# Attention's second product in a cross-attention kernel: matmuls of 256 columns in place of 512

## The chip, the cores and the metric

The kernel runs on one core of a Trainium2 chip. A core has a matrix engine (PE, with its weight loads PEld shown apart), a vector engine (DVE), an activation engine (ACT), a general engine (POOL) and a queue for transfers (SP). Matrix products are written to eight accumulator banks of 128 rows by 512 fp32 columns; ACT and DVE read them from there. The metric is the time of one execution on the device in microseconds (us), the median over runs. Lower is better.

## What is computed

Two batches of 2048 tokens with 640 channels attend to 154 context tokens (77 of text, 77 of an image prompt), with 20 heads of 32 channels. Text and image each have their own keys, values and softmax, and the two outputs are added.

```
q = split_heads(x @ Wq.T)
k, v       = split_heads(text @ Wk.T), split_heads(text @ Wv.T)
k_ip, v_ip = split_heads(ip @ Wk_ip.T), split_heads(ip @ Wv_ip.T)
out = softmax(q k.T / sqrt(32)) v + softmax(q k_ip.T / sqrt(32)) v_ip
return merge_heads(out) @ Wo.T + bo + x
```

All of it is in fp32.

## The kernel before, in words

Four heads of 32 channels fill the 128 rows of a tile, so 20 heads make five groups; with two batches there are ten pairs of batch and group, numbered q = 0 to 9. A pair's 2048 tokens fall into two halves (`sub` 0 and 1) of 1024.

For each half the kernel projects queries (line 194), multiplies them with the keys (line 226), copies the scores from the banks into a large buffer `pb` (ACT, line 238), and does the softmax there: maxima (DVE, line 251), subtraction (line 265), exponential (ACT, line 272), sums (DVE, line 297), division (line 309). Then DVE transposes `pb` in blocks of 32 by 32 (line 316). `pb` has three zones of 1024 tokens: an even q has its halves in zones 0 and 1, an odd q in zones 2 and 1.

When both halves of a pair are transposed, `attend` (line 318) multiplies the probabilities with the values. Text and image tokens stand behind each other, 154 rounded up to 160, that is five blocks of 32 (`NK` = 5). The matmuls use 32 by 32 pieces of PE's array, called squares here: a square is one (r, g) with r the row group of the array that it reads from (which also names the bank) and g the head, which names the 32 output rows. For each block k, all 16 squares (r, g) are issued, each with its own 32 by 32 weights from `v4` and 512 columns of `pb`, 256 of them from each of the pair's two zones. A result adds up over the five k in its bank. That is 80 matmuls an attend, and ten attends. ACT then copies the four banks to `aT` (lines 348 and 352), and PE multiplies with the output weights: for the first batch by a scheme with seven products (lines 464 to 493), for the second by one with products on sums of blocks (line 854, after the last attend).

The order of all work on all engines is written out by hand: a long list of words, one for each step, and each engine takes its instructions in the order of that list. `A.8@1360` is the attend of pair 8 on banks 1, 3, 6 and 0. The list is not touched by the change. Waits between engines are placed by the framework from what each instruction reads and writes.

In the trace every fp32 matmul of the program stands as two weight loads (LDWEIGHTS on PEld) and two matmul records on PE: an attend's 80 matmuls are 160 records, the ten attends 1600. The two are called a square's first and second pass here; both use the same 32 by 32 piece of the array, and both read the same columns.

Of the kernel before, what the change touches and what calls it, by code (L numbers as in the profile page):

```python
# [15 lines left out]
H, D, TEXT = 20, 32, 77  # L16
# [4 lines left out]
def kernel(  # L21
# [25 lines left out]
    nc = tc.nc  # L47
# [3 lines left out]
    G = P // D  # L51
    TB = 512
    NH = 2
    BLK = NH * TB
    NT = BLK // P
    SUB = S // BLK
    NHB = SUB * NH
# [3 lines left out]
    NK = (2 * L + D - 1) // D  # L61
    LP = NK * D
    SCALE = 1.0 / float(D) ** 0.5
    NP = B * NC
# [17 lines left out]
    v4s = [const.tile([P, G, NK, D], F32, name=f"v4_{n}") for n in range(2)]  # L82
# [235 lines left out]
    def attend(q, pa):  # L318

        zones = pb[:, ds(q % 2, SUB)].rearrange("p z n g (k s) -> p (z n) g k s", k=NK)  # L320
        for k in range(NK):
            for r in range(G):
                rows = slice(r * D, (r + 1) * D)
                for g in range(G):
                    nc.tensor.matmul(  # L325
                        pa[r][g * D : (g + 1) * D, :],
                        v4s[q % 2][rows, g, k, :],
                        zones[rows, :, g, k, :],
                        start=(k == 0),
                        stop=(k == NK - 1),  # L330
                    )

    def rows_of_attention(b, c):

# [304 lines left out]
    def emit(word):  # L639
# [8 lines left out]
        elif k == "A":  # L648
            at[name] = banks_at(where)
            attend(x, at[name])  # L650
        elif k == "CA":
            take_attention(x, at[f"A.{x}"])
# [244 lines left out]
```

## Time and profile before

| | |
|---|---|
| time, median of 3 runs | 498.39 us (498.36 to 498.49) |
| span of the profiled execution, first to last instruction | 496.5 us |
| PE busy | 489.3 us (99%) |
| DVE busy | 441.2 us (89%) |
| POOL busy | 403.7 us (81%) |
| ACT busy | 241.9 us (49%) |
| line 325, the attends on PE | 55.2 us busy, 1600 records |
| chain that ended last, PE's share | 91% |

The page gives no other time of the profiled execution than its span; it lies 1.9 us under the median of the timed runs, and what is outside the first and last instruction is taken as unchanged. PE's records have real starts, while their ends are modelled, so the starts are what to read. A row of a table of stretches gives, for each engine, the busy time within the stretch and in brackets how many instructions overlap it; where all stretches begin just before an attend, the number in brackets counts what has started by the stretch's end.

### The profile page before, as it was taken

How to read it: one execution, taken by the hardware profiler on the slowest of the kernel's cores; microseconds unless marked ns; L12 is line 12 of the kernel's file. 1: busy time of each engine (PE TensorE's matmuls, PEld its weight loads, DVE VectorE, ACT ScalarE, POOL GpSimd, SP SyncE). 2: the span in 40 equal slices, each digit the busy share in tenths (PEclk: the TensorE clock that was granted, in tenths of full speed). 3: DMA queues.
4: the chain of work that ended last, by engine and by line, in shares of the span. 5: the costliest groups of instructions: out<-in, count | busy, mean ns of one | idle time of the engine just before them, and what ended most of it. 6: DMA issues, size and time to landing. Idle time of an engine off the chain costs nothing.

```text
span 496.5 us, 9743 instructions
## 1 busy us (share of the span) xinstructions
PE 489.3 (99%) x4114; PEld 288.0 (58%) x4114; DVE 441.2 (89%) x404; ACT 241.9 (49%) x423; POOL 403.7 (81%) x173
## 2 busy tenths in 40 slices
PE   8999999999999999999999999999999999999996
PEld 4658548648647556456655655744766575444442
DVE  0078999999989989998999998899899999999886
ACT  1277557757747567567506635545764443100000
POOL 0079959999989999997995899799599999378770
PEclk9999999999999999999999999999999999999999
DMA  8980542511843735715577078345515012510026
GB/s 291 354 213 20 153 107 71 176 51 36 209 133 89 244 108 172 219 16 164 222 243 237 22 241 309 97 150 185 189 65 160 3 45 64 170 62 24 0 106 232
DMA packets 66956, 70.15 MB, mean 141 GB/s; under 512 B 3680, under 2 KB 46688, under 8 KB 66912
## 3 DMA queue, kind: packets, MB, share of 16 engines
q1 hardware_dynamic: 65648, 67.96, 44.0%
q10 hardware_dynamic: 1264, 1.57, 0.9%
q8 instruction: 32, 0.52, 0.4%
q14 instruction: 12, 0.10, 0.1%
HBM read 58.21 MB, written 11.30 MB: 140 GB/s over the span
## 4 chain that ended last, share of the span: by engine, by line
PE 91%; DVE 6%; DMA 1%; ACT 1%; ACTq 0%; issue 0%; DVEq 0%
PE bank L194 35%; PE bank L854 11%; PE bank L325 11%; PE bank L226 10%; PE bank L133 9%; PE bank L483 9%; PE bank L464 4%; PE bank L493 2%; DVE pb L316 2%; DMA x<-in_x_dram 1%; DVE den L297 1%; DVE mx L251 1%; DVE acc L508 0%; DVE acc L512 0%; ACT pb L238 0%
## 5 line engine op out<-in xcount | busy, mean ns | idle before, releaser
L309 POOL TENSOR_TENSOR pb<-pb,rden 128x1848 f32<-128x1848 f32 (+1 forms) x59 | 172.1, 2938 | 24.0 <-DVE rden L304 21.2
L265 POOL TENSOR_TENSOR pb<-pb,mx 128x1848 f32<-128x1848 f32 (+1 forms) x55 | 162.8, 2977 | 35.4 <-DVE mx L251 35.2
L194 PE MATMUL bank<-x,wq 128*128 128x512 f32 x400 | 178.6, 598 | 0.9 <-DMA wq<-in_L_xattn_Wq_dram 0.6
L251 DVE TENSOR_REDUCE mx<-pb 128x24 f32<-128x1848 f32 (+1 forms) x60 | 109.3, 1841 | 31.5 <-ACT pb L238 31.3
L194 PEld LDWEIGHTS bank<-x,wq 128*128 128x128 f32 x400 | 74.0, 190 | 89.3 <-issue 82.0
L238 ACT COPY pb<-bank 128x462 f32<-128x462 f32 (+1 forms) x240 | 102.0, 537 | 44.5 <-PE bank L226 43.9
L272 ACT ACTIVATE pb<-pb 128x1848 f32<-128x1848 f32 (+1 forms) x60 | 94.3, 1584 | 55.0 <-POOL pb L265 54.2
L297 DVE TENSOR_REDUCE den<-pb 128x24 f32<-128x1848 f32 (+1 forms) x60 | 110.0, 1840 | 5.9 <-ACT pb L272 5.7
L316 DVE STREAM_TRANSPOSE pb<-pb 128x1920 f32<-128x1920 f32 (+1 forms) x60 | 113.9, 1923 | 0.9 <-POOL pb L309 0.9
L226 PEld LDWEIGHTS bank<-kT,qT 32*128 32x128 f32 x1280 | 45.9, 184 | 23.6 <-issue 14.2
L226 PE MATMUL bank<-kT,qT 32*128 32x154 f32 x1280 | 56.5, 305 | 1.0 <-ACT pb L238 0.7
L325 PE MATMUL bank<-pb,v 32*32 32x512 f32 x1600 | 55.2, 597 | 0.1
L204 ACT ACTIVATE qT<-bank 128x512 f32<-128x512 f32 x40 | 23.6, 597 | 50.3 <-PE bank L194 50.3
L133 PE MATMUL bank<-wo_ct,aT 128*128 128x154 f32 x320 | 45.5, 296 | 0.0
L133 PEld LDWEIGHTS bank<-wo_ct,aT 128*128 128x128 f32 x320 | 43.0, 188 | 3.6 <-issue 2.7
L325 PEld LDWEIGHTS bank<-pb,v 32*32 32x32 f32 x1600 | 29.5, 103 | 22.9 <-issue 11.7
L464 PE MATMUL bank<-aT,wo_ct 128*128 128x512 f32 x80 | 36.3, 596 | 0.0
L483 PE MATMUL bank<-aT,wo_ct 128*128 128x256 f32 x128 | 32.8, 389 | 0.0
L802 DVE TENSOR_TENSOR x<-x,bank 128x512 f32<-128x512 f32 x36 | 23.6, 684 | 5.2 <-PE bank L854 4.6
L483 PEld LDWEIGHTS bank<-aT,wo_ct 128*128 128x128 f32 x128 | 23.3, 190 | 6.4 <-issue 3.7
L464 PEld LDWEIGHTS bank<-aT,wo_ct 128*128 128x128 f32 x80 | 15.0, 190 | 17.3 <-issue 17.1
L854 PE MATMUL bank<-pb 128*128 128x512 f32 x48 | 22.1, 593 | 0.0
(74 smaller groups left out, 347.6 us busy)
## 6 DMA issues: line engine op xcount, KB each, us to landing
x<-in_x_dram SPq DMA_DIRECT2D x20, 1280.0 KB, 7.7
out_dram<-acc SPq DMA_DIRECT2D x20, 256.0 KB, 2.6
acc<-in_x_dram SPq DMA_DIRECT2D x16, 256.0 KB, 4.0
x<-in_x_dram SPq DMA_DIRECT2D x15, 256.0 KB, 5.7
out_dram<-x SPq DMA_DIRECT2D x15, 256.0 KB, 2.0
v<-scr SPq DMA_DIRECT2D x40, 80.0 KB, 4.1
wq<-in_L_xattn_Wq_dram SPq DMA_DIRECT2D x9, 320.0 KB, 5.3
aT<-in_L_xattn_Wk_dram SPq DMA_DIRECT2D x5, 512.0 KB, 6.9
```

Of the source, the lines that this page charges most:

```text
L133: nc.tensor.matmul(keys_in(out), loaded[n][:, k, :], cT[:, k, :, t, :], start=(k == 0), stop=(k == NCC - 1))
L194: nc.tensor.matmul(pq, wqs[q % 3][:, k, :], xs[place_of(u, h)][:, k, :], start=(k == 0), stop=(k == NC - 1),)
L226: nc.tensor.matmul(ps[g][:, ts(t, 2 * L)], qTs[(u, h)][g * D : (g + 1) * D, ts(st, P)], kT[g * D : (g + 1) * D, c, b].rearrange("p t l -> ...
L238: nc.scalar.copy(keys_of(u, s)[:, :, g], ps[g][:, : n * 2 * L].rearrange("p (n l) -> p n l", n=n))
L251: nc.vector.tensor_reduce(mx, rows_of(u, s), AX.X, ALU.max, negate=by_rows(u, s))
L265: eng.tensor_tensor(rows_of(u, s), rows_of(u, s), maxs[(u, s)].unsqueeze(3).to_broadcast([P, n, 2, L]), ALU.subtract)
L272: nc.scalar.activation(e, e, AF.Exp)
L297: nc.vector.tensor_reduce(dens[(u, s)], rows_of(u, s), AX.X, ALU.add)
L309: eng.tensor_tensor(rows_of(u, s), rows_of(u, s), rdens[(u, s)].unsqueeze(3).to_broadcast([P, n, 2, L]), ALU.mult)
L316: nc.vector.transpose(p, p)
L325: nc.tensor.matmul(pa[r][g * D : (g + 1) * D, :], v4s[q % 2][rows, g, k, :], zones[rows, :, g, k, :], start=(k == 0), stop=(k == NK - 1),)
L483: nc.tensor.matmul(part, w_of[m][:, kp, op], t_of(m, b, i)[:, kp], start=(op == kp == 0 and m in (1, 2, 5)), stop=(op == 1 and kp == 1 and ...
```

## The change

Only `attend` is changed. A matmul now covers 256 columns in place of 512: one half h of the bank, which is one zone of `pb`. An attend has 160 matmuls in place of 80, over the same columns in all, with the weights of a square given again for the second half. There are three orders. For even q except 8, all 16 squares (r outside, g inside) go on half 0 and then all 16 on half 1, for each k. For odd q it is the same, with r inside and g outside. For q = 8 (`NP - 2`) both halves of one square follow each other before the next square. Only the first matmul of a square in an attend (k = 0, h = 0) starts a new sum in the bank; the second half is opened by it as well.

```
     def attend(q, pa):
         zones = pb[:, ds(q % 2, SUB)].rearrange("p z n g (k s) -> p (z n) g k s", k=NK)
+        span = NHB * TB // G // NH
+        part = SUB * NT // NH
+
+        def square(k, h, r, g):
+            rows = slice(r * D, (r + 1) * D)
+            nc.tensor.matmul(
+                pa[r][g * D : (g + 1) * D, ds(h * span, span)],
+                v4s[q % 2][rows, g, k, :],
+                zones[rows, ds(h * part, part), g, k, :],
+                start=(k == h == 0),
+                stop=(h == NH - 1 and k == NK - 1),
+                skip_group_check=True,
+            )
+
         for k in range(NK):
-            for r in range(G):
-                rows = slice(r * D, (r + 1) * D)
-                for g in range(G):
-                    nc.tensor.matmul(
-                        pa[r][g * D : (g + 1) * D, :],
-                        v4s[q % 2][rows, g, k, :],
-                        zones[rows, :, g, k, :],
-                        start=(k == 0),
-                        stop=(k == NK - 1),
-                    )
+            if q == NP - 2:
+                for r in range(G):
+                    for g in range(G):
+                        for h in range(NH):
+                            square(k, h, r, g)
+                continue
+            for h in range(NH):
+                for r in range(G):
+                    for g in range(G):
+                        square(k, h, *((g, r) if q % 2 else (r, g)))
```

On PE, at the first attend (q = 0, `v_0` holds its values, the banks are named by number), the start of the block k = 0 read before, behind the query projection of line 194:

```order
L194 MATMUL bank_80<-x_97,wq_88 128x512 x5
L325 MATMUL bank_86<-pb,v_0_92 32x512 x4
L325 MATMUL bank_83<-pb,v_0_92 32x512 x4
L325 MATMUL bank_84<-pb,v_0_92 32x512 x4
L325 MATMUL bank_85<-pb,v_0_92 32x512 x4
```

and now, where the matmul is on line 326:

```order
L194 MATMUL bank_80<-x_97,wq_88 128x512 x5
L326 MATMUL bank_86<-pb,v_0_92 32x256 x4
L326 MATMUL bank_83<-pb,v_0_92 32x256 x4
L326 MATMUL bank_84<-pb,v_0_92 32x256 x4
L326 MATMUL bank_85<-pb,v_0_92 32x256 x4
L326 MATMUL bank_86<-pb,v_0_92 32x256 x4
L326 MATMUL bank_83<-pb,v_0_92 32x256 x4
L326 MATMUL bank_84<-pb,v_0_92 32x256 x4
L326 MATMUL bank_85<-pb,v_0_92 32x256 x4
```

Four squares (the four g) on each bank came once for a block k; now the round over the four banks comes twice, once for each half. What stands before the attend and behind it is the same.

At the attend of q = 8, behind an output product (line 464 before, 479 now), the block k = 0 read before:

```order
L464 MATMUL bank_86<-aT,wo_ct 128x512 x5
L325 MATMUL bank_80<-pb,v_0_92 32x512 x4
L325 MATMUL bank_82<-pb,v_0_92 32x512 x4
L325 MATMUL bank_85<-pb,v_0_92 32x512 x4
L325 MATMUL bank_79<-pb,v_0_92 32x512 x4
```

and now:

```order
L479 MATMUL bank_86<-aT,wo_ct 128x512 x5
L326 MATMUL bank_80<-pb,v_0_92 32x256 x8
L326 MATMUL bank_82<-pb,v_0_92 32x256 x8
L326 MATMUL bank_85<-pb,v_0_92 32x256 x8
L326 MATMUL bank_79<-pb,v_0_92 32x256 x8
```

Each bank is visited once for a block k as before, with eight matmuls in place of four: two in a row on each of its four squares.

## Prediction

> **What bounds the kernel now.** I read the page first, then the waits of PE, then stretches.
>
> ```profile
> span 496.5 us, 9743 instructions
> PE 489.3 (99%) x4114; PEld 288.0 (58%) x4114; DVE 441.2 (89%) x404; ACT 241.9 (49%) x423; POOL 403.7 (81%) x173
> PE 91%; DVE 6%; DMA 1%; ACT 1%; ACTq 0%; issue 0%; DVEq 0%
> L325 PE MATMUL bank<-pb,v 32*32 32x512 f32 x1600 | 55.2, 597 | 0.1
> ```
>
> PE is busy 99% of the span and holds 91% of the chain that ended last. Its modelled ends can hide waits, so I ask what ended its idle times; the first row of PE's waits is the longest, and of the attends' weight loads only three waited for a transpose:
>
> ```profile
> PE bank L546 <- DVE pb L544: 1.1, 1, 1.1
> PEld bank L325 <- DVE pb L316: 2.0, 3, 1.0
> ```
>
> By stretches, from the first attend to the last one, and within it the two behind the attend of q = 8 (columns: PE, PEld, DVE, ACT, POOL busy; clock; transfers):
>
> ```profile
> 69.00:426.40 357.40, 357.23 (x3407) 217.84 (x3406) 340.31 (x282) 208.07 (x356) 323.37 (x126) 1.00 0.46 141
> 391.00:399.00 8.00, 8.00 (x192) 5.47 (x169) 7.90 (x11) 5.29 (x9) 7.77 (x5) 1.00 0.02 5
> 399.00:426.40 27.40, 27.34 (x126) 17.08 (x124) 27.23 (x27) 8.79 (x13) 26.20 (x15) 1.00 0.24 78
> ```
>
> PE idles 0.17 us of 357.40, at full clock. So whatever an attend gains or loses on PE moves everything behind it one for one. From 399.00 DVE is full too (27.23 of 27.40), and the chain of waits goes over to it there; but PE is as full, so a later PE has nothing to be absorbed in.
>
> **What sets the time of an attend.** First the price of one pass. In the chain of waits, 20 records of 512 columns take 8.58 us and 8 of 256 columns 1.73 us, that is 0.429 and 0.216 each: a pass costs its columns, with nothing fixed.
>
> ```profile
> 46.82 8.58 PE bank L194 x20
> 365.89 1.73 PE bank L483 x8
> ```
>
> An attend has 160 passes on 16 squares, so 10 sets of 16; at 0.429 these are 4.29 us. Measured is more, from PE's timeline:
>
> ```profile
> 69.03 5.52 PE L325 MATMUL bank<-pb,v 32*32 32x512 f32 x160
> 74.48 1.07 PE L226 MATMUL bank<-kT,qT 32*128 32x154 f32 x24
> ```
>
> From its first start to the next line's are 5.45 us, 1.16 over the ten sets. The stretches of line 325 show where that goes (PE, then PEld; in brackets the starts so far; all counted from 69.02):
>
> ```profile
> 69.02:69.47 0.45, 0.43 (x16) 0.31 (x32) 1.00 0.00 0
> 69.02:69.60 0.58, 0.56 (x25) 0.42 (x33) 1.00 0.00 0
> 69.02:69.90 0.88, 0.86 (x32) 0.42 (x33) 1.00 0.00 0
> 69.02:70.10 1.08, 1.06 (x33) 0.52 (x34) 1.00 0.00 0
> 69.02:70.12 1.10, 1.08 (x34) 0.54 (x35) 1.00 0.00 0
> 69.02:70.33 1.31, 1.29 (x47) 0.74 (x60) 1.00 0.05 14
> 69.02:71.17 2.15, 2.13 (x66) 1.12 (x68) 1.00 0.24 66
> 69.02:71.19 2.17, 2.15 (x67) 1.14 (x69) 1.00 0.25 69
> 69.02:72.26 3.24, 3.23 (x101) 1.85 (x103) 1.00 0.54 158
> 69.02:73.34 4.32, 4.30 (x135) 2.61 (x137) 1.00 0.71 198
> 69.02:73.95 4.93, 4.92 (x159) 2.91 (x160) 1.00 0.74 200
> 69.02:73.97 4.95, 4.93 (x160) 2.91 (x160) 1.00 0.73 200
> ```
>
> By 69.47 sixteen passes and 32 weight loads have started: I read the first pass of all 16 squares, with the weights of the second passes loaded behind. By 69.90 the 16 second passes have started too. Then nothing, though 15 squares have room for their next weights: 33 loads and 32 matmuls are in, and only when the first square has ended both passes (2 x 0.429, at 69.92) does one more matmul start, and the 34th start comes at 70.11. So PE looks ahead over 16 squares and no further. From then the starts come in steps: 34, 67, 101 and 135 by 70.12, 71.19, 72.26 and 73.34, that is 34 starts, or **17 squares, every 1.073 us**. One step is a square's two passes, 0.858, plus a **pause of 0.215** until the square 17 places behind it has got in. Within a step squares follow each other closely (13 starts from 70.12 to 70.33, 0.0165 each). Check: first late start 1.075 after the first; three more steps, 4.295 (square 68 of 0 to 79); eleven squares at 0.0165, 4.48; the last square's second pass 0.429 and 0.022 later, 4.93. The table has the last start between 73.95 and 73.97, 4.93 after 69.03. Behind the last start the pass (0.429) and 0.088 go by until line 226.
>
> **The change part by part.** Columns stay the same: twice as many passes of half the length. What doubles is the number of squares that pass through a lookahead that counts instructions. The weights of all added squares are loaded again; the loads hide, as before, behind the passes (33 were in while 32 passes ran).
>
> *Nine attends (all but q = 8).* A step of 17 squares is now 2 x 0.216 + 0.215 = 0.647, and there are 160 squares. First late start: 1.075 less 2 x 0.213 = 0.649. Eight more steps reach square 153 at 5.825; six squares at 0.0165, 5.92; the last one's second pass 0.216 + 0.022 later, **6.16** against 4.93, so +1.23. Behind it the shorter last pass gives back 0.429 - 0.216 = 0.213. Net **+1.02 each, +9.17 in all**. Steps of issue do not bind: 17 squares at 0.0165 are 0.28 of 0.647. The swapped order for odd q changes which square is 17 places behind, not that it is a different one, so I price it at nothing.
>
> *The attend of q = 8.* Two squares in a row use the same piece, so four passes queue on it, 4 x 0.216 = 0.864, and 16 squares of lookahead fill only 8 pieces. A step is 0.864 + 0.215 = 1.079 and moves 18 squares. First late start at about 1.08; seven more steps reach square 144 at 8.63; 14 squares, 8.86; the last piece's fourth pass starts 3 x 0.216 + 0.022 later, 9.53. Against 4.93 that is +4.60, less 0.213: **+4.39**.
>
> *Waits.* An even q's half 0 needs only one zone, so 16 squares can start before the other half's transpose. Three waits of 2.0 us together, which include 0.5 that PE needs to empty before any attend, leave some 0.5 us that this could save at most; I take 0. The transfers of `v4` are waited for by the first squares as before. What is late next: the copies out of the banks and line 226, each by what the attend adds.
>
> *Sum.* 9.17 + 4.39 = 13.56. On the span 496.5 it gives 510.1; with the 1.9 us outside it, 498.39 + 13.56 = **512.0**.
>
> *Bounds.* The unknown is the pause at 256 columns. Its lower bound is nothing: then 0.649 + 8 x 0.647 loses 9 x 0.215, and an attend is 0.92 faster than before (break-even of a normal attend at 0.102). Its upper bound is the full 0.215, seen in all steps at both places where it can be read (the end of the first square and three steps later). I take 0.215, since it begins when a pass has ended and holds no column time.
>
> [...]
>
> **Rivals.**
>
> *A fixed price for each set of 16 passes.* The 1.16 us over ten sets may be 0.116 a set, whatever its order. Twenty sets of 0.332 are 6.64, +1.19 an attend, all ten alike: +11.9, **510.3**. For it: it needs no lookahead. Against: the steps of 34 starts, not 32. Chance 0.15, with all cases in which q = 8 costs about as much as the others.
>
> *The lookahead holds columns, not instructions (faster).* Place: the stop at 69.60 to 69.92. If what is full there is a store of pending columns, 32 squares of 256 fit, and a step of 34 squares costs 4 x 0.216 + 0.215 = 1.079, as 17 do now. Then only the last pass is shorter: 10 x -0.213 = -2.1, **496.3**. It decides as soon as the pause per 17 squares falls under 0.102; with none at all it would be 9 us. Against: 33 loads, 64 instructions and one, is a count of instructions. Chance 0.11.
>
> *The pair of q = 8 blocks what stands behind it.* If a second square on a busy piece stops all issue until the first has ended, each of the 80 pairs costs 2 x 0.216 or more: 34.6 us in place of 5.45, +29, **537**. For it: the trace never has two matmuls in a row on one piece. Against: second passes did wait 0.429 while squares behind them started. Chance 0.10.
>
> *One start every 0.0165 is all that binds.* 320 starts take 5.3: +0.37 - 0.213, +0.16 an attend, **500**. Against: by 69.47 and 69.60 starts come closer (9 in 0.13). Chance 0.08. That the change does nothing measurable: 0.05.
>
> **How the numbers follow.** The forecast has 0.51, with a range of its own from 509 to 515. Within about 0.2% (1 us) this kernel cannot be told from unchanged; that is the 0.05. Faster is the 0.11; slower the rest, 0.84. The range leaves out the blocked pair and the faster case: from the rival of starts, 500, to where the pair of q = 8 costs some 12 us in place of 4.4, **500 to 520**.
>
> **What would show it.** Right: nine attends of 6.5 us from first start to the next line's; in them 34 starts every 0.65 us; q = 8 at about 9.8; PE still idle under 1 us from the first attend to the last. Wrong: attends under 5.45 (lookahead in columns); all ten at 6.6 (a price a set); q = 8 above 20 (blocked); odd q apart from even q (the swapped order costs something that I have at nothing); or PE waiting for DVE between attends, by which part of the loss would be absorbed.

## The result and the profile after

The changed kernel takes **538.16 us** (median of six runs), the kernel before 498.38 on the same chip: a ratio of 1.0795, with a 95% interval of 1.0775 to 1.0814. The ratio leaves out one run of 545.83 us, in which the granted clock was lower (0.981, against 0.989 to 0.994 in the others). The changed kernel is slower by some 40 us. The forecast was 512.0, with a range of 500 to 520: the direction was right, the size missed by more than the range.

The page of the changed kernel, in the profiled execution (536.72 us, with the span below):

```profile
span 534.8 us, 12947 instructions
PE 509.8 (95%) x5714; PEld 311.1 (58%) x5714; DVE 439.6 (82%) x404; ACT 242.5 (45%) x423; POOL 403.8 (76%) x173
q8 instruction: 45, 0.74, 0.6%
PE 94%; issue 3%; DMA 1%; ACT 0%; ACTq 0%; DVE 0%
L326 PE MATMUL bank<-pb,v 32*32 32x256 f32 x3200 | 73.6, 390 | 16.5 <-issue 16.4
```

PE still sets the end, but it is no longer busy all the time, and the attends' row now has idle time, 16.4 us of it with the releaser "issue": PE stood still and waited for nothing that the profile names. Before, that row had 0.1. The first rows of PE's waits say the same with counts (us in total, times, longest):

```profile
PE bank L326 <- issue: 16.4, 11, 3.2
PE bank L226 <- issue: 1.4, 2, 0.7
```

PE's timeline shows where they lie. In such a row the x counts the starts up to the next stop, and the idle time in brackets stands ahead of the row. It runs from the modelled end of the last pass; from start to start a stop is up to 0.4 us longer. The attends of q = 3, 5, 6, 7, 8 and 9:

```profile
188.67 4.02 PE L326 MATMUL bank<-pb,v 32*32 32x256 f32 x192
192.93 2.75 PE L326 MATMUL bank<-pb,v 32*32 32x256 f32 x128 [0.24 <-issue]
...
272.41 2.81 PE L326 MATMUL bank<-pb,v 32*32 32x256 f32 x135
277.05 2.74 PE L326 MATMUL bank<-pb,v 32*32 32x256 f32 x128 [1.83 <-issue]
281.33 1.43 PE L326 MATMUL bank<-pb,v 32*32 32x256 f32 x57 [1.53 <-issue]
...
320.33 4.68 PE L326 MATMUL bank<-pb,v 32*32 32x256 f32 x229
328.18 2.08 PE L326 MATMUL bank<-pb,v 32*32 32x256 f32 x91 [3.18 <-issue]
...
366.92 4.08 PE L326 MATMUL bank<-pb,v 32*32 32x256 f32 x201
373.55 4.01 PE L326 MATMUL bank<-pb,v 32*32 32x256 f32 x119 [2.55 <-issue]
...
417.25 9.99 PE L326 MATMUL bank<-pb,v 32*32 32x256 f32 x320
...
457.18 3.95 PE L326 MATMUL bank<-pb,v 32*32 32x256 f32 x184
463.95 2.75 PE L326 MATMUL bank<-pb,v 32*32 32x256 f32 x128 [2.82 <-issue]
467.68 0.63 PE L326 MATMUL bank<-pb,v 32*32 32x256 f32 x8 [0.98 <-issue]
```

Every normal attend has one or two such stops; q = 8 has none. Where two follow within an attend, they are 128 starts apart (q = 5: after 135 and 263), and a start on PE goes with a weight load (5714 of each on the page), so they are 256 instructions apart. Counted in the order of PE's instructions through the whole program (loads, matmuls, and the waits that stand as instructions of their own), the stops of all attends lie on one lattice of 256: each lies 193 or 194 instructions past a multiple of 256. The page's queue q8, of the kind "instruction", has packets of 16 KB (0.74 MB in 45). Before, the row was

```profile
q8 instruction: 32, 0.52, 0.4%
```

The change adds 3200 instructions (1600 matmuls and 1600 loads) and 13 packets. If a packet holds 256, these are 3328; run 5 below, with 6400 instructions and 25 packets more, gives just 256. The trace also has the time of every packet. Before each of the 13 stops of the two rows of waits one packet starts, and PE goes on 2.31 to 2.64 us after that start: at q = 6 the packet starts at 325.70 and PE goes on at 328.18. So the reading is: **PE runs out of instructions at the end of a block of 256 and waits until the next one has come.**

Between the stops the kernel does what the forecast said. Stretches of line 326 from the start of q = 3 (PE, with the starts so far in brackets):

```profile
188.66:189.33 0.67, 0.66 (x34) 1.00 0.00 0
188.66:189.96 1.30, 1.29 (x67) 1.00 0.00 0
188.66:191.91 3.25, 3.24 (x170) 1.00 0.02 5
188.66:192.90 4.24, 4.02 (x192) 1.00 0.01 4
```

34 starts come every 0.65, as forecast (0.647), up to 170; then the count stays at 192 until 192.93.

Where the 38.3 us between the two spans (534.8 and 496.5) are: the ten attends, each from its first start to the next line's, are longer by 36.0 together (7.2 to 8.1 us for q = 0 to 4 and 9.9 to 11.8 for q = 5 to 9, against 5.5). Of that 13.6 is the forecast's sum, and **22.4 are stops and what they bring**. The other 2.3 lie between the attends: a stop just behind q = 0 (1.05) and a low clock behind q = 9 (1.7), less 0.4 by which two other stretches are shorter.

### The profile page after: what moved, and what is told of

Same layout as the page of the kernel before. It is cut to its first block, busy times and chain, and to the rows that moved or that the text cites. A ratio compares the mean times of both kernels' runs of the same rounds, so it can differ in the third digit from the quotient of the medians.

```text
span 534.8 us, 12947 instructions
## 1 busy us (share of the span) xinstructions
PE 509.8 (95%) x5714; PEld 311.1 (58%) x5714; DVE 439.6 (82%) x404; ACT 242.5 (45%) x423; POOL 403.8 (76%) x173
## 4 chain that ended last, share of the span: by engine, by line
PE 94%; issue 3%; DMA 1%; ACT 0%; ACTq 0%; DVE 0%
PE bank L194 32%; PE bank L326 14%; PE bank L869 11%; PE bank L226 10%; PE bank L498 10%; PE bank L133 8%; PE bank L479 7%; PE bank L508 3%; DMA wq<-in_L_xattn_Wq_dram 1%; ACT pb L238 0%; DVE x L817 0%; ACTq L166 0%; ACTq L537 0%; ACT aT L367 0%; ACTq L907 0%
## 5 line engine op out<-in xcount | busy, mean ns | idle before, releaser
L326 PE MATMUL bank<-pb,v 32*32 32x256 f32 x3200 | 73.6, 390 | 16.5 <-issue 16.4
L326 PEld LDWEIGHTS bank<-pb,v 32*32 32x32 f32 x3200 | 51.5, 104 | 39.4 <-issue 26.5
L367 ACT COPY aT<-bank 128x256 f32<-128x256 f32 x40 | 11.5, 410 | 42.2 <-PE bank L326 42.2
L479 PEld LDWEIGHTS bank<-aT,wo_ct 128*128 128x128 f32 x80 | 15.1, 192 | 17.8 <-issue 17.5
## 6 DMA issues: line engine op xcount, KB each, us to landing
aT<-in_L_xattn_Wk_dram SPq DMA_DIRECT2D x5, 512.0 KB, 7.0
```

The lines of the kernel that those rows point to most:

```text
L326: nc.tensor.matmul(pa[r][g * D : (g + 1) * D, ds(h * span, span)], v4s[q % 2][rows, g, k, :], zones[rows, ds(h * part, part), g, k, :], st ...
```

## The experiments

The theory after the result was: PE uses up instructions faster than blocks of 256 come. The rivals: the orders (swapped squares, or the pairs of q = 8) cost what was missed; or the lookahead of the forecast is itself wrong.

**1. One order for all.** All ten attends in the plain order of even q, without the swap and the pairs:

```
-            if q == NP - 2:
...
             for h in range(NH):
                 for r in range(G):
                     for g in range(G):
-                        square(k, h, *((g, r) if q % 2 else (r, g)))
+                        square(k, h, r, g)
```

> The change with one order for all ten attends (both halves outside, r outside g), so neither the pair order of q = 8 nor the swapped order of odd q. Theory (lookahead of 16 squares, and on top of it PE out of instructions at every 256th instruction): the last start of an attend comes 6.16 us after the first when it meets no such edge, q = 8 drops from 9.6 us to about 6.2 plus an edge of 0.5 to 3.5; odd q as in the changed kernel but for the edges; total 533 to 540 us. Rival (the pair order of q = 8 blocks what is behind it and is the cause of the loss): 508 to 511 us. Rival (the swapped order is the cause): odd attends alike to even ones, 520 or less.

Measured: 539.83 us, ratio 1.0802 (1.073 to 1.0874). The odd q lost their swap and kept their stops at the same counts (q = 5 after 135 and 263, q = 7 after 201). The attend of q = 8 lost its pairs, went from a last start at 9.62 to 7.57, and got a stop:

```profile
425.27 5.91 PE L326 MATMUL bank<-pb,v 32*32 32x256 f32 x278
431.87 1.34 PE L326 MATMUL bank<-pb,v 32*32 32x256 f32 x42 [0.70 <-issue]
```

So neither order is the cause.

**2. Pairs everywhere.** The order of q = 8 for all q:

```
         for k in range(NK):
...
+            for r in range(G):
+                for g in range(G):
+                    for h in range(NH):
+                        square(k, h, r, g)
```

> 256 columns, the two halves of a square right behind each other in all ten attends. Lookahead theory: 18 squares per 4 x 0.216 + 0.215 = 1.08 us, last start 9.5 us after the first in each attend, and since 640 instructions then take 9.8 us (a block of 256 in 3.9 us), few stops at the edges of blocks: 498.4 + 10 x 4.39 = 542 us, up to 548. Rival (a pair blocks what is behind it): 35 us an attend, 790 us. Rival (stops come with the number of instructions whatever their pace): 560 us or more.

Measured: 555.69 us, ratio 1.1149 (1.1127 to 1.1172). The attends of q = 1 to 4 and 8 have no stop, and a last start 9.56 (q = 8: 9.62) after the first, where 9.53 was forecast for q = 8. The timeline of q = 1, then of q = 5:

```profile
112.62 9.93 PE L326 MATMUL bank<-pb,v 32*32 32x256 f32 x320
...
284.28 4.45 PE L326 MATMUL bank<-pb,v 32*32 32x256 f32 x135
289.71 4.38 PE L326 MATMUL bank<-pb,v 32*32 32x256 f32 x128 [0.98 <-issue]
296.45 4.02 PE L326 MATMUL bank<-pb,v 32*32 32x256 f32 x57 [2.36 <-issue]
```

The pair does not block what stands behind it. The time lies 7.7 us above the 548 that was expected at most: even at this slower pace (36 starts in 1.08 us) five attends still stop. It lies under the 560 of the rival by which stops come whatever the pace.

**3. Pairs without more instructions.** The kernel before, 512 columns, with the blocks k ordered so that two matmuls in a row use one square:

```
-        for k in range(NK):
-            for r in range(G):
+        for k, r, g in ((k, r, g) for ks in ((0, 1), (2, 3), (4,)) for r in range(G) for g in range(G) for k in ks):
                 rows = slice(r * D, (r + 1) * D)
-                for g in range(G):
...
```

> 512 columns and 80 matmuls an attend as before, but blocks k = 0 and 1 of a square right behind each other, then 2 and 3, then 4 alone: the same instructions in another order. Lookahead theory: 18 squares per 4 x 0.429 + 0.215 = 1.93 us, last start 8.3 us after the first in place of 4.93, no stops at edges: 498.4 + 34 = 532 us. Rival (a fixed price for each set of 16 passes): 498.4 us, no change.

Measured: 531.29 us, ratio 1.066 (1.0639 to 1.0681). Each attend has its last start 8.30 to 8.35 after the first, as worked out; there is no stop in it, and the page's row has no idle time:

```profile
L324 PE MATMUL bank<-pb,v 32*32 32x512 f32 x1600 | 89.0, 593 | 0.0
```

The same instructions in another order cost 33 us. That shows the lookahead by itself, and rules out a fixed price for each set of 16 passes, by which this kernel would have stayed at 498.

**4. Half the columns.** Only h = 0 in every attend; the second half of each result is left out, so it has 80 matmuls of 256 columns.

```
         for k in range(NK):
...
+            for r in range(G):
+                for g in range(G):
+                    square(k, 0, r, g)
```

> Leaves out the second half of every attend: 80 matmuls of 256 columns, half of the attention's result is not computed. Instructions as many as before. Lookahead theory with a pause of 0.215 us that does not depend on columns: steps of 34 starts every 0.647 us, last start 3.01 us after the first, 3.31 to the next line: 10 x -2.14, 477 us, and up to 485 with stops at edges of blocks (97 instructions a us). If the pause shrank with the columns to 0.108: steps of 0.54, last start 2.6, 473 us.

Measured: 496.83 us, ratio 0.996 (0.9941 to 0.9978). In nine attends the last start comes 3.01 after the first, as worked out with the pause of 0.215, where a pause that shrank with the columns would have given 2.6: the pause was the same 0.215 at 256 columns as at 512. The total was missed. The attends gave back 17.5 us together, and 16 of them were lost again between them, mostly because PE now waits: it idles 9.06 of the 357.40 us below, against 0.17 before. The granted clock is also a little lower (0.99). A stretch from the first attend on as in the prediction, the chain's shares, and the first row of PE's waits:

```profile
69.00:426.40 357.40, 348.34 (x3508) 218.14 (x3508) 342.32 (x285) 207.45 (x356) 323.20 (x126) 0.99 0.46 142
...
PE 49%; DVE 23%; POOL 18%; ACT 4%; issue 3%; DMA 1%; ACTq 0%; DVEq 0%; POOLq 0%
...
PE bank L226 <- ACT qT L204: 3.1, 4, 1.7
```

PE's share of the chain fell from 91% to 49%. So one for one holds for a loss on PE and not for a gain: DVE (342.32 of 357.40 busy) and POOL stand close behind.

**5. Quarters.** Four matmuls of 128 columns in place of two of 256, plain order (`span` and `part` halved, h over four). That doubles the instructions again.

> 128 columns: 320 matmuls, 1280 instructions an attend, all 16 squares on each quarter in turn. Lookahead alone: steps of 2 x 0.109 + 0.215 = 0.433 us for 17 squares, last start 8.2 us after the first, 528 us in all. With fetching of instructions in blocks of 256 that takes some 3.7 us a block when one follows the other: five blocks an attend, 14 to 20 us each, 590 to 650 us in all, with stops 128 starts apart.

Measured: 643.99 us, ratio 1.2922 (1.2893 to 1.2951), with 70 packets of instructions: 25 more than with 256 columns, and 25 x 256 = 6400 is just what was added. The attend of q = 3:

```profile
223.81 1.90 PE L326 MATMUL bank<-pb,v 32*32 32x128 f32 x128
226.94 1.90 PE L326 MATMUL bank<-pb,v 32*32 32x128 f32 x128 [1.22 <-issue]
230.39 2.82 PE L326 MATMUL bank<-pb,v 32*32 32x128 f32 x128 [1.55 <-issue]
233.84 2.82 PE L326 MATMUL bank<-pb,v 32*32 32x128 f32 x128 [0.64 <-issue]
237.30 2.82 PE L326 MATMUL bank<-pb,v 32*32 32x128 f32 x128 [0.63 <-issue]
```

A stop after every 128 starts, and a block every 3.45 us (230.39, 233.84, 237.30), whatever PE does in between: from the third row on the same 128 starts take 2.82 in place of 1.90 (the page has a granted clock of 0.6 for 224.8 to 240.9), but the step is the same. The changed kernel's trace shows such a step in its parts: behind the stop of q = 3 the next packet starts 1.13 us after PE has gone on (192.93, then 194.06), and PE goes on again 2.3 us after that (196.38), 3.45 together. In other attends of this run the step is 3.73 or 4.00, or more where other transfers run, and never less than 3.45.

**6. One attend alone.** 256 columns only for q = 6 (plain order), 512 for the rest.

> Only the attend of q = 6 in 256 columns, the nine others as before. Lookahead alone: +1.02 us, 499.4 us. With stops at edges of blocks of 256 instructions: one to two edges fall in it, 0.5 to 3.5 us in all: 500 to 503 us; none in the other nine attends.

Measured: 502.4 us, ratio 1.0104 (1.0057 to 1.0152), within what was expected. The stops come with the one attend:

```profile
303.40 3.49 PE L326 MATMUL bank<-pb,v 32*32 32x256 f32 x166
308.19 2.75 PE L326 MATMUL bank<-pb,v 32*32 32x256 f32 x128 [1.29 <-issue]
311.64 0.71 PE L326 MATMUL bank<-pb,v 32*32 32x256 f32 x26 [0.70 <-issue]
```

They lie after 166 and 294 starts, not after 229 as in the changed kernel: fewer instructions stand ahead, so the lattice has moved. From 308.19 to 311.64 are again 3.45 us.

**7. The lattice moved.** In the changed kernel, 32 small matmuls (128 instructions, half a block) ahead of everything.

```
+    for _ in range(32):
+        nc.tensor.matmul(banks[0][:D, :D], warm[:D, :D], warm[:D, :D], start=True, stop=True)
```

> The changed kernel with 32 small matmuls (128 instructions) added at the start, where PE waits for transfers. If the stops lie at every 256th instruction of PE, each moves 64 starts earlier in its attend: from the 193rd start to the 129th in q = 0, from 135 and 263 to 71 and 199 in q = 5, from 229 to 165 in q = 6, from 201 to 137 in q = 7, from 184 and 312 to 120 and 248 in q = 9. Total 530 to 545 us. If they hang on data or on other engines, they stay where they are.

Measured: 536.59 us, ratio 1.0767 (1.0701 to 1.0834). All stops lie on the lattice moved by 64 starts: q = 6 now after 165 (it was 229), q = 7 after 137 (201), q = 5 after 199 (135 or 263), q = 9 after 248 (184):

```profile
322.80 3.48 PE L326 MATMUL bank<-pb,v 32*32 32x256 f32 x165
327.30 2.74 PE L326 MATMUL bank<-pb,v 32*32 32x256 f32 x128 [1.02 <-issue]
...
368.12 2.99 PE L326 MATMUL bank<-pb,v 32*32 32x256 f32 x137
373.20 4.05 PE L326 MATMUL bank<-pb,v 32*32 32x256 f32 x128 [2.09 <-issue]
```

Nothing of an attend's work changed but its place in PE's instructions, and the stops went with that place. This is the run that settles the cause. Not every edge of the lattice is a stop: the first one within an attend is passed, in this kernel as in the changed one. In this kernel two attends (q = 0 and 4) also passed the second; their first edge lay within the first four starts. So the lattice is where it was expected, but the stops expected after 129 (q = 0), 71 (q = 5) and 120 starts (q = 9) did not come.

**8. Without competing loads.** The changed kernel without the 20 loads of x (1280 KB each) of the second batch, which is then computed on what lies there (`KEEP` is empty).

```
+        if step_of(u)[0] not in KEEP:
+            return
         nc.sync.dma_start(
...
```

> The changed kernel without the 20 loads of x blocks (1280 KB each) for the second batch, whose result is not computed from its own tokens. If the longer stops of q = 5 to 9 (1.4 to 3.6 us, against 0.5 to 1.7 before) are instruction blocks that queue behind these loads, they fall to 0.5 to 1.7 us and the total to 526 to 531 us. If the fetch does not mind other transfers: 535 to 540 us.

Measured: 528.61 us, ratio 1.0607 (1.0577 to 1.0637), so some 9 us less than the changed kernel. The long stops of q = 6 and q = 7 (3.18 and 2.55 idle) are short:

```profile
320.53 4.77 PE L329 MATMUL bank<-pb,v 32*32 32x256 f32 x233
325.69 2.04 PE L329 MATMUL bank<-pb,v 32*32 32x256 f32 x87 [0.39 <-issue]
...
364.40 4.50 PE L329 MATMUL bank<-pb,v 32*32 32x256 f32 x206
369.46 2.64 PE L329 MATMUL bank<-pb,v 32*32 32x256 f32 x114 [0.56 <-issue]
...
458.47 4.41 PE L329 MATMUL bank<-pb,v 32*32 32x256 f32 x131 [2.84 <-issue]
```

The counts are 4 or 5 starts higher than in the changed kernel, as they would be on the same lattice if 8 to 10 of PE's instructions, waits for these loads, were missing ahead (an estimate from the counts; the whole program has 37 instructions fewer, 12910 against 12947). So in the changed kernel the block came later while x was loaded. That is also what the stretches of the changed kernel show at q = 6 (the last three columns are the clock, the share of the transfer engines and GB/s):

```profile
324.00:325.00 1.00, 1.00 (x56) 0.56 (x33) 0.97 (x3) 0.36 (x1) 1.00 (x2) 1.00 1.03 401
325.00:328.00 3.00, 0.01 (x1) 0.00 (x0) 0.76 (x3) 0.00 (x0) 2.59 (x1) 1.00 0.29 107
```

The transfer engines are full just ahead of the stop (still 1.07 from 325.00 to 325.70, then 0.11 to 326.80), and the packet of instructions starts at 325.70, as the load of x ends. At q = 9 the stop stays as it was (2.84, the last row above, behind 189 starts), so the loads of x are not its cause. The changed kernel's trace shows others there, the loads of `acc` and `res` (lines 834 and 838, 1024 and 256 KB), which are in run 8 as well:

```profile
459.00:461.50 2.50, 2.13 (x108) 1.30 (x85) 2.50 (x4) 0.00 (x0) 0.00 (x0) 1.00 1.03 401
461.50:463.90 2.40, 0.00 (x0) 0.00 (x0) 1.46 (x7) 0.00 (x0) 0.45 (x1) 1.00 0.09 28
```

Here the packet starts at 461.64, as these loads end, and PE goes on 2.31 us later. That looks like the same delay behind other loads, but no run left these out.

**9. The swap alone.** The kernel before, 512 columns, with g outside and r inside for all q.

> 512 columns as before, but r inside and g outside in all ten attends, the order that the change gives to odd q. If the order of the 16 squares within a round is free, as the forecast has it: 498.4 us, within 0.2%, and a last start 4.93 us after the first. If squares of one g (or of four r) in a row get in each other's way, the last start comes later and the total is up to several us more.

Measured: 498.85 us against 498.39, ratio 1.0007 (0.9998 to 1.0017): no difference. The swapped order cost nothing.

**10. A fifth of the change.** 256 columns only for k = 0 of each attend, so 96 matmuls in place of 80; the blocks k = 1 to 4 are as before.

```
         for k in range(NK):
+            if k == 0:
+                for h in range(NH):
+                    for r in range(G):
+                        for g in range(G):
+                            square(k, h, r, g)
+                continue
...
```

> 256 columns for the first block k = 0 alone, 512 for the other four: 96 matmuls, 384 instructions an attend. Lookahead theory: 16 more squares of half the width, last start 5.14 us after the first in place of 4.93, the last pass as long as before: 10 x 0.21, 500.5 us. 384 instructions in 5.7 us are 68 a us, about the pace of a block of 256 every 3.7 us, so stops at edges are few and short: up to 504 us.

Measured: 505.62 us, ratio 1.0148 (1.0098 to 1.0198), and 502.67 to 507.5 from run to run, so a little above what was expected. Eight attends have no stop of note and, read at q = 2, a last start 5.1 to 5.2 after the first; q = 5 has a short one (0.68 from start to start) and q = 9 one of 2.15 from start to start, between its passes of 512 columns:

```profile
435.86 1.06 PE L345 MATMUL bank<-pb,v 32*32 32x512 f32 x8 [1.56 <-issue]
```

At 512 columns 128 starts take 4.04 us (128/34 x 1.073), close to the 3.45 to 4.00 that a block took in quiet stretches of run 5, so the reserve is thin there too.

## Why the prediction was right and wrong

**PE bounds the kernel, and what an attend loses moves the end one for one: right.** The spans differ by 38.3 us, the attends by 36.0. That it would hold for a gain as well was not shown by a full PE alone: by run 4 it does not.

**The lookahead of 16 squares: right, in structure and size.** Steps of 34 starts every 0.65 (0.647 forecast); the last start of the five normal attends with one stop at full clock is 6.01 to 6.03 after the first, with the stop taken off from start to start (6.16); q = 8 at 9.62 (9.53). The unknown, the pause at 256 columns, was taken at its upper bound 0.215, and runs 3, 4 and 5 agree. So the terms 9.17 and 4.39 hold within some 0.15 us an attend.

**The swapped order at nothing, and the waits for transposes at nothing: right** (run 9 for the first, and the steps of 0.65 at q = 3, which has that order; the attends' wait for transposes is no part of the 36.0).

**The step that failed is "Steps of issue do not bind".** It compared 17 squares with the rate of starts within one step, 0.0165, and so took for granted that the instructions are there to be issued. Over a whole attend they are not. What has to be compared is the time of a block of 256 instructions, that is 128 starts:

| | 128 starts take, us | a block comes every, us (measured in run 5, taken for all rows) |
|---|---|---|
| before, 512 columns (34 starts in 1.073) | 4.04 | 3.45 to 4.00 |
| pairs of 256 (36 in 1.079) | 3.84 | same |
| changed, 256 columns (34 in 0.647) | 2.44 | same |
| quarters, 128 columns (34 in 0.431) | 1.62 | same |

The first two rows are in balance, as nearly all attends of 512 columns and half of those in pairs have no stop; the changed one loses 0.5 to 1.9 us, from start to start, at most of the edges that the reserve does not cover, and 2.2 to 3.6 where the block is delayed more. Since an attend holds 640 instructions, 2.5 blocks, that is one or two stops for each. In all: 22.4 us within the attends and 1.05 behind the first, with the low clock below. The line of the forecast that would have told is "PE still idle under 1 us from the first attend to the last": PE waits 16.4 + 1.4 us for issue.

The profile of before held two parts of the sum that was not done: 0.52 MB in 32 packets on the instruction queue, beside PE's 4114 loads and 4114 matmuls, give the block (257 instructions a packet, as an estimate), and 320 instructions in 5.45 us the pace. The time of a block was not to be read there, as PE did not wait for one. The traces show the stops 256 instructions apart. They also show a reserve of about one further block, as an estimate: in the nine attends of the changed kernel that have stops, PE passes the first edge without idle time each time, and the second only at q = 1 (after 150 starts). What holds this reserve, and how large it can be, was not shown.

**The rivals.** The blocked pair gave 537, close to the measured time, and is wrong all the same: q = 8 took 9.9 us, not 35, and pairs everywhere gave 556 where blocking would have added hundreds. The price per set falls with run 3, the lookahead in columns with the attends' steps, and the rate of 0.0165 with the same steps. None of the four named the supply of instructions, and so the range was too narrow on the slow side.

**Left open:** why a block's time in quiet stretches of run 5 is 3.45, 3.73 or 4.00, and how a block's packet meets other transfers. Run 8 shows that the loads of x lengthen the wait (3.18 and 2.55 us with them, 0.39 and 0.56 without). Since PE goes on 2.31 to 2.64 us after a packet's start however long the stop, the delay lies ahead of that start (at q = 6 and 9 until the running load ends); why the packet has to wait there is not shown.

## What to carry to other kernels

When a change cuts the same work into more and shorter instructions, compare two times for a block of PE's instructions, 256 of them in this kernel: how long it takes to run, and how long the next block takes to come (3.45 to 4.00 us in quiet stretches of run 5; while x was loaded, stops were up to 3.2 us long). Here the matmuls of 256 columns on 32 by 32 squares, with a weight load for each pass, needed a block every 2.44 us and those of 512 every 4.04. And before making the bounding engine faster, look how close the next one is: in run 4, with DVE and POOL close behind, 16 of 17.5 us were lost again.

## What the runs showed of the hardware that was not expected

**PE stopped at the edges of its instruction blocks**, up to 3.2 us long in the changed kernel, and the profile calls that only "issue". The place of a stop went with how many instructions stand ahead in the whole program, so an edit far away moved it (run 7: 128 more instructions at the start moved the stops by 64 starts).

**The granted clock was low behind some stops.** The attend of q = 7 in the changed kernel, behind a stop of 2.55 us, and that of q = 6, behind one of 3.18 (PE, PEld, DVE, ACT, POOL, clock, transfers):

```profile
373.50:377.40 3.90, 3.85 (x119) 2.57 (x119) 1.78 (x2) 0.00 (x0) 1.97 (x1) 0.60 0.55 144
328.00:330.20 2.20, 2.02 (x92) 1.31 (x91) 0.00 (x0) 0.47 (x1) 0.00 (x0) 1.00 0.04 7
```

At a granted clock of 0.60, 119 starts take 3.9 us; at 1.00, 92 take 2.0, so 119 would take 2.6, as an estimate. So at q = 7 the low clock cost 1.3 us on top of the stop. Behind q = 9 the clock is low too (0.50 from 469.90 to 473.20), and four passes of 512 columns take 3.00 us in place of 1.98 before:

```profile
469.00 3.00 PE L869 MATMUL bank<-x,wo_ct 128*128 128x512 f32 x4 [0.69 <-ACT aT L367]
```

There the waits just ahead are short (0.98 and 0.69); behind the stop of 2.82, 6 us earlier, the clock was at 1.00 (460.00 to 467.90).

At q = 7 the clock was 0.50 from 374.30 to 377.60. The length of a single stop does not decide it: in the changed kernel that stop was 2.55 us long, while right behind those of 2.82 and 3.18 the clock stayed at 1.00, and in run 8 the ten passes of line 197 behind a stop of 1.81 us at q = 5 took 6.26 us, against 4.56 elsewhere, with a clock of 0.8 on the page for 276.9 to 290.1. What decides it was not worked out.
